# Powers of a strictly triangular matrix in a chunked linear-attention kernel: products over the part that the mask leaves

## The chip, the cores and the metric

The kernel runs on one core of one Trainium2 chip. The metric is device time in microseconds of one execution of the whole program. TensorE (PE) multiplies, VectorE (DVE) and ScalarE (ACT) move results out of PSUM and do elementwise work, GpSimd (POOL) and SyncE (SP) mostly start transfers.

## The reference

Two transformer-like layers over 4096 tokens of 256 features, fp32, one sequence:

```python
x = x + _L0_attn_ref(_layernorm(x), ...)   # linear attention with two memories
x = x + _L0_ffn_ref(_layernorm(x), ...)    # top 2 of 8 experts, 256 -> 1024 -> 256
x = x + _L1_attn_ref(_layernorm(x), ...)   # RWKV-like recurrence and channel mix
x = x + _L1_ffn_ref(_layernorm(x), ...)    # gated feed-forward, 1024 wide
```

The change is in the first attention. There each token t updates two 64x64 memories H (a fast one and a slow one, decayed by alpha) with the delta rule, and reads them with its query:

```python
d_fast = kv - k_t[:, :, None] * jnp.einsum('bk,bkv->bv', k_t, fH)[:, None, :]
fH = fast_alpha * fH + (1 - fast_alpha) * d_fast
```

## The kernel before

The attention is cut into 8 blocks of 512 tokens and each block into 4 chunks of 128 tokens: 32 chunks. Inside a chunk, token t needs what earlier tokens of the chunk wrote, which is a triangular system (1 - L) W = Y for each of the two memories (f = 0, 1). L is a 128x128 matrix, strictly lower triangular: `lower` (L595) multiplies the Gram matrix of the keys by `ncmaskT`, which is zero on and above the diagonal. The system is solved by doubling: Y becomes Y + L^(2^j) Y for j = 0 to 6, and L^(2^j) is squared between the steps. L^(2^j) has non-zero entries only where the row number is at least 2^j above the column number.

L and Y of one f lie side by side in one tile LY of 256 columns: half 0 is L, half 1 is Y. A step j of a chunk is:

- `turn(j)` (L605): PE transposes L of both f into PSUM (L608); `keep_turn` (L610) lets ACT copy it to SBUF as LT (L612, 128x256 for both f).
- `factor(j, f)` (L614): for j below 5 one product per f gives L L and L Y together, 256 columns (L619), with LT as the loaded side. For j = 5 there are two products of 128 columns: L Y (L624), and the transposed L^64 directly, with L as the loaded side and LT streaming (L627), since j = 6 needs no L itself. For j = 6 only L Y (L624).
- `keep_factor(j)` (L629): ACT copies the squared L to the next LY (L641), or, for j = 5, the transposed L^64 to an LT tile (L644); then DVE adds old and new Y (L645). For j = 6 DVE writes the sum to DP (L633).

After step 6 come a transpose of DP (`flip_d`, L650), products with the memory (`write` L663, `carry` L673) and the reads of the memory (`read` L689, L693). L609 to L612 and L639 to L645 take their tiles from rotating pools (LT 5 buffers, LY 7).

The order of the work is written out. A `Plan` collects steps with a time and a rank, sorts them, and PE, ACT, DVE and SP run exactly that order, each as one queue. A chunk begins every PACE = 7 units and its step j stands at 4 j:

```python
t = PACE * (NT * b + i) + 4 * j
for f in range(2):
    plan.at(t + f / 2, FEED, lambda j=j, f=f: factor(j, f))
plan.at(t + 1, OUT, lambda j=j: keep_factor(j))
```

So four chunks are in flight, and products of different chunks alternate on PE: between `factor(j, 0)` and `factor(j, 1)` of a chunk there is often a `turn` of another chunk. In the same queue stand the projections of later blocks (`project`; among them L442, 64 output rows, and L402, L414, L434, L453), the ends of earlier blocks (`finish`; among them the transposes L747, L781, L809 and the product L821 that contracts over 64 rows) and the routing (`route`).

Towards the end of the attention the first four slots of 256 tokens of the experts are worked on in the same plan (`full_slot`, L1088): products L1141 and L1155, then DVE adds the bias into a tile y (`add`, L1160 to L1163, two buffers) and SP stores it (L1166). The other experts follow, then the second layer.

Of the kernel before, what the change touches and what calls it, by code (L numbers as in the profile page):

```python
# [8 lines left out]
F32 = mybir.dt.float32  # L9
# [3 lines left out]
ALU = mybir.AluOpType  # L13
AX = mybir.AxisListType

P = 128
# [34 lines left out]
def mk_seq_kernel(ctx: ExitStack, tc: tile.TileContext, a: dict, out: bass.AP):  # L51
# [88 lines left out]
    def bcast(ap, shape):  # L140
        return ap.to_broadcast(shape)
# [124 lines left out]
    for q in range(3):  # L266
        t = ac.tile([P, P], F32, name=f"h{q}")
        nc.gpsimd.memset(t, 0.0)
        HS.append(t)


    TT = S // P
    sel = ac.tile([P, 2, TT, NE], F32, name="sel")
# [64 lines left out]
    ROUTE, LAST = 91, 81  # L338
    plan = Plan()
    zs = [{} for _ in range(NB)]  # L340
    memory = {"ns": None, "n": 0}

    def moments(b, z, key, i):
        if i == 0:
# [24 lines left out]
    def project(b):  # L369
# [131 lines left out]
        def starts():  # L501

            ly = z["LY"] = a2.tile([P, NT, 2, 2, P], F32, tag="LY0", name=f"LY0_{b}")
            nc.vector.tensor_tensor(
                ly[:, :, :, 1, :DS], bcast(z["KQ"][:, :, 0:1, :], [P, NT, 2, DS]),
                bcast(y["kd"].unsqueeze(3), [P, NT, 2, DS]), ALU.mult,
            )

        def values():
            nc.vector.tensor_tensor(  # L510
                z["LY"][:, :, :, 1, DS:], bcast(z["v"].unsqueeze(2), [P, NT, 2, DS]),
                bcast(z["us"].unsqueeze(3), [P, NT, 2, DS]), ALU.mult,
            )

# [51 lines left out]
    def factors(b, i):  # L566

        z = zs[b]
        y = z["c", i] = {}
        t_ = f"{b}_{i}"  # L570

        def flip():
            y["pk"] = psb([P, 2, P], f"pk_{t_}")
            for g in range(2):
                nc.tensor.transpose(
                    y["pk"][:, g, :], z["KQ"][:, i, 2 * g : 2 * g + 2, :].rearrange("p g d -> p (g d)"),
                    ident,
                )

        def keep():  # L580
            y["kq"] = a2.tile([P, 2, P], F32, tag="kqT", name=f"kqT_{t_}")
            nc.scalar.copy(y["kq"], y["pk"])

        def decayed():
            y["qT"] = a2.tile([P, P], F32, tag="qT", name=f"qT_{t_}", bufs=8)
            nc.vector.tensor_tensor(y["qT"], y["pk"][:, 1, :], qdec, ALU.mult)

        def gram():
            y["pg"] = psb([P, 2, P], f"pg_{t_}")
            nc.tensor.matmul(  # L590
                y["pg"].rearrange("p g t -> p (g t)"), y["kq"][:, 0, :],
                y["kq"].rearrange("p g t -> p (g t)"), start=True, stop=True,
            )

        def lower():  # L595
            for f in range(2):
                nc.vector.scalar_tensor_tensor(
                    z["LY"][:, i, f, 0, :], y["pg"][:, 0, :], z["us"][:, i, f : f + 1],
                    ncmaskT[:, f, :], ALU.mult, ALU.mult,
                )  # L600
            y["G"] = a2.tile([P, 2, P], F32, tag="G", name=f"G_{t_}", bufs=8)
            nc.vector.tensor_tensor(y["G"], bcast(y["pg"][:, 1:2, :], [P, 2, P]), cmask, ALU.mult)
            y["L"] = z["LY"][:, i]

        def turn(j):  # L605
            y["pt"] = psb([P, 2, P], f"pt{j}_{t_}")
            for f in range(2):
                nc.tensor.transpose(y["pt"][:, f, :], y["L"][:, f, 0, :], ident)  # L608

        def keep_turn(j):  # L610
            y["LT"] = a2.tile([P, 2, P], F32, tag="LT", name=f"LT{j}_{t_}", bufs=5)
            nc.scalar.copy(y["LT"], y["pt"])  # L612

        def factor(j, f):  # L614
            if f == 0:
                y["p"] = psa([P, 2, 2, P], f"pf{j}_{t_}")
            p, L, LT = y["p"], y["L"], y["LT"]
            if j < 5:
                nc.tensor.matmul(  # L619
                    p[:, f].rearrange("p g t -> p (g t)"), LT[:, f, :],  # L620
                    L[:, f].rearrange("p g t -> p (g t)"), start=True, stop=True,
                )
                return
            nc.tensor.matmul(p[:, f, 1, :], LT[:, f, :], L[:, f, 1, :], start=True, stop=True)  # L624
            if j == 5:

                nc.tensor.matmul(p[:, f, 0, :], L[:, f, 0, :], LT[:, f, :], start=True, stop=True)  # L627

        def keep_factor(j):  # L629
            p, L = y["p"], y["L"]  # L630
            if j == 6:
                y["DP"] = a2.tile([P, 2, 2, DS], F32, tag="DP", name=f"DP_{t_}", bufs=3)
                nc.vector.tensor_tensor(  # L633
                    y["DP"].rearrange("p g f d -> p f g d"),
                    p[:, :, 1, :].rearrange("p f (g d) -> p f g d", g=2),
                    L[:, :, 1, :].rearrange("p f (g d) -> p f g d", g=2), ALU.add,
                )
                return
            N = a2.tile([P, 2, 2, P], F32, tag="LY", name=f"LY{j + 1}_{t_}", bufs=7)  # L639
            if j < 5:  # L640
                nc.scalar.copy(N[:, :, 0, :], p[:, :, 0, :])  # L641
            else:
                y["LT"] = a2.tile([P, 2, P], F32, tag="LT", name=f"LT{j + 1}_{t_}", bufs=5)
                nc.scalar.copy(y["LT"], p[:, :, 0, :])  # L644
            nc.vector.tensor_tensor(N[:, :, 1, :], p[:, :, 1, :], L[:, :, 1, :], ALU.add)  # L645
            y["L"] = N

        def flip_d():
            y["pd"] = psb([P, P], f"pd_{t_}")
            nc.tensor.transpose(y["pd"], y["DP"][:, 0].rearrange("p f d -> p (f d)"), ident)  # L650

        def keep_d():
            y["dT"] = a2.tile([P, P], F32, tag="dT", name=f"dT_{t_}")
            nc.scalar.copy(y["dT"], y["pd"])


        def write():
            if i == 0:
                z["W"] = a2.tile([P, NT, 2, DS], F32, tag="W", name=f"W_{b}")
                z["pP"] = ps.tile([P, NT, 2, DS], F32, tag="p", name=f"pP_{b}", bufs=1)  # L660
            y["H"] = HS[memory["n"] % 3]
            y["pW"] = psc([P, P], f"pW_{t_}")
            nc.tensor.matmul(y["pW"], y["dT"], y["H"], start=True, stop=True)  # L663

        def keep_write():
            nc.vector.tensor_tensor(
                z["W"][:, i].rearrange("p f d -> p (f d)"), y["pW"],
                y["DP"][:, 1].rearrange("p f d -> p (f d)"), ALU.add,
            )

        def carry():
            y["pH"] = psc([P, P], f"pH_{t_}")
            nc.tensor.matmul(  # L673
                y["pH"], z["ke"][:, i].rearrange("p f d -> p (f d)"),
                z["W"][:, i].rearrange("p f d -> p (f d)"), start=True, stop=True,
            )

        def keep_carry():
            memory["n"] += 1
            N = HS[memory["n"] % 3]  # L680
            for f in range(2):
                o = slice(f * DS, (f + 1) * DS)
                nc.vector.scalar_tensor_tensor(
                    N[o, o], y["H"][o, o], aend[o, :], y["pH"][o, o], ALU.mult, ALU.add
                )

        def read():
            pP = z["pP"][:, i]
            nc.tensor.matmul(  # L689
                pP.rearrange("p f d -> p (f d)"), y["qT"], y["H"], start=True, stop=False  # L690
            )
            for f in range(2):
                nc.tensor.matmul(  # L693
                    pP[:, f, :], y["G"][:, f, :], z["W"][:, i, f, :], start=False, stop=(f == 1)
                )

        for t, rank, fn in (
            (-13, MIX, flip), (-12.75, OUT, keep), (-12.5, OUT, decayed), (-9, MIX, gram),
            (-8.75, OUT, lower), (-6, MIX, lambda: turn(0)), (-5.75, OUT, lambda: keep_turn(0)),
            (26, MIX, flip_d), (26.25, OUT, keep_d), (31, MIX, write), (31.25, OUT, keep_write),  # L700
            (33, MIX, carry), (33.25, OUT, keep_carry), (34, MIX, read),
        ):
            plan.at(PACE * (NT * b + i) + t, rank, fn)
        for j in range(7):
# [4 lines that stand above are left out]
            if j < 5:  # L709
                plan.at(t + 2.5, MIX, lambda j=j: turn(j + 1))  # L710
                plan.at(t + 2.75, OUT, lambda j=j: keep_turn(j + 1))
# [376 lines left out]
    def full_slot(k, ups, downs):  # L1088
# [70 lines left out]

        def add(i):  # L1160
            if i == 0:
                z["y"] = me.tile([P, NS2, D], F32, tag="y", name=f"y_f{k}", bufs=2)
            nc.vector.tensor_tensor(z["y"][:, i, :], z["px"], z["b2"], ALU.add)  # L1163

        def store():
# [1109 lines left out]
```

## Time and profile before

| what | value |
|---|---|
| three timed runs | 2042.1, 2045.76 and 2046.39 us, median 2045.76 |
| the profiled execution | 2045.78 us, span from first to last instruction 2044.3 us |
| mean granted TensorE clock in the span | 0.983 |
| L619, first to last start | 41.6 to 451.3 us |
| L624, first to last start | 61.9 to 462.6 us |
| L608, first to last start | 33.5 to 452.4 us |

The profile counts what each engine was busy with. Rows of PE are matmuls, rows of PEld the loads of their stationary side. "128*128 128x256" on a PE row means 128 contraction rows and 128 output rows, and 256 columns that stream; "64*128" contracts over 64 rows, "128*64" makes 64 output rows. A line number is that of the kernel before. Busy times of PE overlap, so the timeline's starts tell more than its durations.

### The profile page before, as it was taken

The numbers are of one execution on the slowest core, as the hardware profiler recorded it, in microseconds if no ns is written. First come the engines' busy times: TensorE is split into PE (matmuls) and PEld (weight loads), VectorE is DVE, ScalarE is ACT, GpSimd is POOL, SyncE is SP. The second block draws the span as 40 slices with busy tenths as digits, with TensorE's granted clock in tenths as the row PEclk, the third lists the DMA queues.
The fourth block names the chain that finished last, engine by engine and source line by source line (L and its number), as shares of the span: only waits on it lengthen the run. The fifth ranks groups of instructions, "written<-read, shape, count | busy, mean of one in ns | idle before, by whom it ended". The sixth has DMA issues, their size and how long they took to land. (4 is left out here: it accounts for less than half of the span.)

```text
span 2044.3 us, 27834 instructions
## 1 busy us (share of the span) xinstructions
PE 1951.9 (95%) x9879; PEld 1656.1 (81%) x9879; DVE 1244.0 (61%) x3013; ACT 1016.1 (50%) x1918; POOL 437.8 (21%) x523
## 2 busy tenths in 40 slices
PE   6999999988899999999997999999999999999998
PEld 4888777777677888888886888888888888888887
DVE  4677888876333435564635768687676876754342
ACT  3665555433222223454534656577565675744342
POOL 1000222222300012121112223232323322122121
PEclk8999999988999999999998999999999999999999
DMA  9999300023477677554433555555565555555585
GB/s 316 342 343 343 110 32 32 32 84 102 168 260 266 227 252 249 178 178 150 147 124 84 109 118 119 114 135 103 113 135 103 134 111 118 109 114 119 102 179 105
DMA packets 328856, 314.86 MB, mean 154 GB/s; under 512 B 18177, under 2 KB 308609, under 8 KB 328705
## 3 DMA queue, kind: packets, MB, share of 16 engines
q1 hardware_dynamic: 158624, 187.61, 28.1%
q0 software_dynamic: 170080, 125.33, 27.9%
q8 instruction: 83, 1.36, 0.3%
q14 instruction: 69, 0.56, 0.1%
HBM read 215.64 MB, written 97.26 MB: 153 GB/s over the span
## 5 line engine op out<-in xcount | busy, mean ns | idle before, releaser
L1086 ACT ACTIVATE hT<-peh,b 128x256 f32<-128x256 f32 x248 | 115.6, 473 | 291.3 <-PE peh L1359 285.8
L1359 PE MATMUL peh<-xgT,w 128*128 128x256 f32 x992 | 229.2, 385 | 8.6 <-DVE y L1381 6.5
L1373 PE MATMUL peo<-w,hT 128*128 128x256 f32 x992 | 224.9, 379 | 0.0
L1359 PEld LDWEIGHTS peh<-xgT,w 128*128 128x128 f32 x992 | 189.2, 193 | 38.7 <-DVE y L1381 9.4
L1932 PE MATMUL psh<-h_hi,part 128*128 128x512 f32 x512 | 211.1, 412 | 0.0
L1932 PE MATMUL psh<-sh_hi,part 128*128 128x512 f32 x512 | 209.2, 409 | 0.0
L1373 PEld LDWEIGHTS peo<-w,hT 128*128 128x128 f32 x992 | 186.7, 190 | 24.4
L2045 DVE TENSOR_TENSOR sh_lo<-hf_sh,sh_hi 128x512 fp32r<-128x512 f32 x128 | 88.3, 690 | 186.3 <-ACT sh_hi L2044 186.3
L1932 PE MATMUL psh<-h_lo,part 128*128 128x512 f32 x512 | 200.5, 392 | 0.0
L1932 PE MATMUL psh<-sh_lo,part 128*128 128x512 f32 x512 | 200.2, 391 | 0.0
L2039 ACT ACTIVATE hf_sh<-psh,vec 128x512 f32<-128x512 f32 x128 | 87.8, 686 | 225.8 <-PE psh L1932 225.4
L619 PE MATMUL pf<-LY,LT 128*128 128x256 f32 x640 | 181.1, 386 | 3.4 <-DVE LY L645 2.2
L645 DVE TENSOR_TENSOR LY<-pf,LY 128x256 f32<-128x256 f32 x192 | 79.0, 417 | 77.4 <-ACT LY L641 50.2
L619 PEld LDWEIGHTS pf<-LY,LT 128*128 128x128 f32 x640 | 106.2, 191 | 22.2 <-issue 6.3
L1827 PE MATMUL pcm<-xcT,w_cm 128*128 128x256 f32 x512 | 120.9, 379 | 0.0
L1860 PE MATMUL pcp<-k,w_cp 128*128 128x256 f32 x512 | 120.9, 379 | 0.0
L612 ACT COPY LT<-pt 128x256 f32<-128x256 f32 x192 | 71.4, 372 | 87.7 <-PE pt L608 79.2
L1932 PEld LDWEIGHTS psh<-h_lo,part 128*128 128x128 f32 x512 | 96.3, 188 | 20.1 <-DVE h_lo L2045 0.4
L1932 PEld LDWEIGHTS psh<-sh_lo,part 128*128 128x128 f32 x512 | 96.3, 188 | 19.7
L1932 PEld LDWEIGHTS psh<-sh_hi,part 128*128 128x128 f32 x512 | 96.3, 188 | 19.5
L1932 PEld LDWEIGHTS psh<-h_hi,part 128*128 128x128 f32 x512 | 96.3, 188 | 19.4
L1860 PEld LDWEIGHTS pcp<-k,w_cp 128*128 128x128 f32 x512 | 97.0, 189 | 14.9
(421 smaller groups left out, 4186.4 us busy)
## 6 DMA issues: line engine op xcount, KB each, us to landing
w<-in_w_dram SPq DMA_DIRECT2D x62, 1024.0 KB
xe_d<-zero SPq DMA_DIRECT2D x32, 1024.0 KB
ys_d<-zero SPq DMA_DIRECT2D x32, 1024.0 KB
part<-in_h1T_dram POOLq DMA_DIRECT2D x64, 512.0 KB
part<-in_h2T_dram POOLq DMA_DIRECT2D x64, 512.0 KB
w_f<-in_w_dram SPq DMA_DIRECT2D x8, 1024.0 KB
part<-in_w1T_dram POOLq DMA_DIRECT2D x32, 256.0 KB
part<-in_w2T_dram POOLq DMA_DIRECT2D x32, 256.0 KB
```

Of the source, the lines that this page charges most:

```text
L612: nc.scalar.copy(y["LT"], y["pt"])
L619: nc.tensor.matmul(p[:, f].rearrange("p g t -> p (g t)"), LT[:, f, :], L[:, f].rearrange("p g t -> p (g t)"), start=True, stop=True,)
L645: nc.vector.tensor_tensor(N[:, :, 1, :], p[:, :, 1, :], L[:, :, 1, :], ALU.add)
L1086: nc.scalar.activation(out, x, AF.Gelu_apprx_tanh, bias=bias)
L1359: nc.tensor.matmul(z["ph", h], z["w1"][:, c, h * P : (h + 1) * P], z["xT"][:, c, :], start=(c == 0), stop=(c == 1),)
L1373: nc.tensor.matmul(z["px"], z["hT"][:, h, i * P : (i + 1) * P], z["w2"][:, h, :], start=(h == 0), stop=(h == NF - 1),)
L1827: nc.tensor.matmul(pk[:, u, :], w_cm[:, c, j * P : (j + 1) * P], z["xnT"][:, c, :], start=(c == 0), stop=(c == 1),)
L1860: nc.tensor.matmul(z["pv"][:, c, :], w_cp[:, j, c * P : (c + 1) * P], z["k2"][:, g, h, u, :], start=(half == 0 and q == 0), stop=(half == ...
L1932: nc.tensor.matmul(pp, w, x[u][:, k, :], start=(k == 0 and u == 0), stop=(k == kk - 1 and u == 1))
L2039: nc.scalar.activation(h, z[nm, j], AF.Gelu, scale=col(nm, j))
L2045: nc.vector.tensor_tensor(lo[:, j, :], h, hi[:, j, :].bitcast(F32), ALU.subtract)
```

## The change

Products with a power of L leave out rows and columns that are zero. `wide(j)` is how many leading columns of L^(2^j) may be non-zero: 128 for j = 0 to 2, then 120, 112, 96, 64. LY now has Y in half 0 and L in half 1, so that the columns to be left out lie at the end. The transposed L^64 has only its upper right quarter non-zero: j = 5 computes that quarter alone (64x64), and ACT copies it into one of three lasting tiles QS whose left halves are zeroed once by POOL. In exchange for their room the tile y of `full_slot` has one buffer instead of two. The core of the diff:

```diff
+    QS = []
+    for q in range(3):
+        t = ac.tile([P // 2, 2, P], F32, name=f"q{q}")
+        nc.gpsimd.memset(t[:, :, : P // 2], 0.0)
+        QS.append(t)
...
+        def wide(j):
+            return P - 2**j if j > 2 else P
+
         def turn(j):
             y["pt"] = psb([P, 2, P], f"pt{j}_{t_}")
             for f in range(2):
-                nc.tensor.transpose(y["pt"][:, f, :], y["L"][:, f, 0, :], ident)
+                nc.tensor.transpose(y["pt"][: wide(j), f, :], y["L"][:, f, 1, : wide(j)], ident)
...
-            nc.scalar.copy(y["LT"], y["pt"])
+            nc.scalar.copy(y["LT"][: wide(j)], y["pt"][: wide(j)])
...
-            p, L, LT = y["p"], y["L"], y["LT"]
+            p, L, LT, k = y["p"], y["L"], y["LT"], wide(j)
             if j < 5:
+                n = P + wide(j + 1)
                 nc.tensor.matmul(
-                    p[:, f].rearrange("p g t -> p (g t)"), LT[:, f, :],
-                    L[:, f].rearrange("p g t -> p (g t)"), start=True, stop=True,
+                    p[:, f].rearrange("p g t -> p (g t)")[:, :n], LT[:k, f, :],
+                    L[:k, f].rearrange("p g t -> p (g t)")[:, :n], start=True, stop=True,
                 )
                 return
-            nc.tensor.matmul(p[:, f, 1, :], LT[:, f, :], L[:, f, 1, :], start=True, stop=True)
+            nc.tensor.matmul(p[:, f, 0, :], LT[:k, f, :], L[:k, f, 0, :], start=True, stop=True)
             if j == 5:
 
-                nc.tensor.matmul(p[:, f, 0, :], L[:, f, 0, :], LT[:, f, :], start=True, stop=True)
+                h = P // 2
+                nc.tensor.matmul(
+                    p[:h, f, 1, :h], L[:k, f, 1, :h], LT[:k, f, h:], start=True, stop=True
+                )
...
             if j < 5:
-                nc.scalar.copy(N[:, :, 0, :], p[:, :, 0, :])
+                nc.scalar.copy(N[:, :, 1, : wide(j + 1)], p[:, :, 1, : wide(j + 1)])
             else:
-                y["LT"] = a2.tile([P, 2, P], F32, tag="LT", name=f"LT{j + 1}_{t_}", bufs=5)
-                nc.scalar.copy(y["LT"], p[:, :, 0, :])
-            nc.vector.tensor_tensor(N[:, :, 1, :], p[:, :, 1, :], L[:, :, 1, :], ALU.add)
+                memory["q"] = memory["q"] % len(QS) + 1
+                y["LT"] = QS[memory["q"] - 1]
+                nc.scalar.copy(y["LT"][:, :, P // 2 :], p[: P // 2, :, 1, : P // 2])
+            nc.vector.tensor_tensor(N[:, :, 0, :], p[:, :, 0, :], L[:, :, 0, :], ALU.add)
...
-                z["y"] = me.tile([P, NS2, D], F32, tag="y", name=f"y_f{k}", bufs=2)
+                z["y"] = me.tile([P, NS2, D], F32, tag="y", name=f"y_f{k}")
```

The other edits swap the halves of LY in `starts`, `values`, `lower` and the last step of `keep_factor`.

More of the change, by code (lines that the diff above doesn't have):

```diff
@@ L340, in mk_seq_kernel @@
     zs = [{} for _ in range(NB)]
-    memory = {"ns": None, "n": 0}
+    memory = {"ns": None, "n": 0, "q": 0}
     def moments(b, z, key, i):
@@ L504, in starts @@
             nc.vector.tensor_tensor(
-                ly[:, :, :, 1, :DS], bcast(z["KQ"][:, :, 0:1, :], [P, NT, 2, DS]),
+                ly[:, :, :, 0, :DS], bcast(z["KQ"][:, :, 0:1, :], [P, NT, 2, DS]),
                 bcast(y["kd"].unsqueeze(3), [P, NT, 2, DS]), ALU.mult,
@@ L510, in values @@
             nc.vector.tensor_tensor(
-                z["LY"][:, :, :, 1, DS:], bcast(z["v"].unsqueeze(2), [P, NT, 2, DS]),
+                z["LY"][:, :, :, 0, DS:], bcast(z["v"].unsqueeze(2), [P, NT, 2, DS]),
                 bcast(z["us"].unsqueeze(3), [P, NT, 2, DS]), ALU.mult,
@@ L597, in lower @@
                 nc.vector.scalar_tensor_tensor(
-                    z["LY"][:, i, f, 0, :], y["pg"][:, 0, :], z["us"][:, i, f : f + 1],
+                    z["LY"][:, i, f, 1, :], y["pg"][:, 0, :], z["us"][:, i, f : f + 1],
                     ncmaskT[:, f, :], ALU.mult, ALU.mult,
@@ L634, in keep_factor @@
                     y["DP"].rearrange("p g f d -> p f g d"),
-                    p[:, :, 1, :].rearrange("p f (g d) -> p f g d", g=2),
-                    L[:, :, 1, :].rearrange("p f (g d) -> p f g d", g=2), ALU.add,
+                    p[:, :, 0, :].rearrange("p f (g d) -> p f g d", g=2),
+                    L[:, :, 0, :].rearrange("p f (g d) -> p f g d", g=2), ALU.add,
                 )
```

## The prediction

> **What bounds the kernel now.** I read the page first, then the busy times by stretch, then PE's timeline.
>
> ```profile
> span 2044.3 us, 27834 instructions
> PE 1951.9 (95%) x9879; PEld 1656.1 (81%) x9879; DVE 1244.0 (61%) x3013; ACT 1016.1 (50%) x1918; POOL 437.8 (21%) x523
> PE   6999999988899999999997999999999999999998
> PEclk8999999988999999999998999999999999999999
> ```
>
> A slice is 51 us. The lines that the change edits run from about 40 to 465 us (first and last start of L619, L624, L627): slices 1 to 9, with PE at nine tenths in most. The chain of waits only begins at 1086.65 us and so never shows this stage; but what follows it is the experts' work, PE nearly full, fed from results of this stage, so I take its lateness to be handed on whole. Busy times by stretch (columns: length, busy us and count of PE, weight loads, DVE, ACT, POOL, clock, DMA share, GB/s):
>
> ```profile
> 100.00:200.00 100.00, 97.38 (x611) 82.80 (x610) 74.54 (x230) 60.01 (x149) 8.67 (x10) 1.00 1.04 343
> 200.00:300.00 100.00, 93.95 (x578) 77.49 (x576) 79.43 (x276) 56.33 (x137) 23.16 (x23) 1.00 0.25 87
> 300.00:400.00 100.00, 93.23 (x594) 78.65 (x593) 82.43 (x281) 50.19 (x131) 22.45 (x23) 1.00 0.09 33
> ```
>
> PE leads at a full granted clock; DVE is second, ACT has room. So the stage is to be priced in PE's time from one start to the next. The timeline gives that; its first column is the start, and a PE record is longer than PE's step, since matmuls overlap. An fp32 product stands as two matmuls (L619: 640 records for 320 products), a transpose as one.
>
> ```profile
> 243.09 0.60 PE L619 MATMUL pf<-LY,LT 128*128 128x256 f32 x2
> 243.53 0.38 PE L663 MATMUL pW<-h,dT 128*128 128x128 f32 x2
> 243.75 0.39 PE L624 MATMUL pf<-LY,LT 128*128 128x128 f32 x2
> 243.97 0.38 PE L608 MATMUL pt<-ident,LY 128*128 128x128 f32 x2
> 244.19 0.39 PE L624 MATMUL pf<-LY,LT 128*128 128x128 f32 x2
> ```
>
> A matmul over 256 columns takes 0.216 us (0.44/2), over 128 columns 0.11 (0.22/2): 0.84 ns per column. The weights load meanwhile.
>
> **The price that the diff hides.** Two kinds of product are new in shape: j=6 now contracts over 64 rows, and the second product of j=5 makes 64 output rows. The kernel already has one of each: L821 contracts over 64 rows ("64*128"), L442 makes 64 rows ("128*64").
>
> ```profile
> 206.10 0.39 PE L627 MATMUL pf<-LT,LY 128*128 128x128 f32 x2
> 206.41 1.13 PE L821 MATMUL px<-w_o,oT 64*128 64x256 f32 x4
> 207.47 0.70 PE L619 MATMUL pf<-LY,LT 128*128 128x256 f32 x2
> 208.01 0.38 PE L608 MATMUL pt<-ident,LY 128*128 128x128 f32 x2
> ```
>
> L627 to L821: 0.316 instead of 0.22, so 0.094 more on entry. Four L821 take 1.06 instead of 0.864: the first is 0.104 longer (its record 480 ns, the median 376), as if its weights had not been loaded ahead, and 0.09 goes before L619 may start. L619, two matmuls, takes 0.54 instead of 0.43: again 0.104. **A visit to 64 rows costs 0.39 us.**
>
> ```profile
> 83.14 0.39 PE L624 MATMUL pf<-LY,LT 128*128 128x128 f32 x2
> 83.46 1.07 PE L442 MATMUL pn<-hn,w_nm 128*64 128x512 f32 x2
> 84.46 0.70 PE L619 MATMUL pf<-LY,LT 128*128 128x256 f32 x2
> 85.00 0.38 PE L608 MATMUL pt<-ident,LY 128*128 128x128 f32 x2
> ```
>
> Here entry costs 0.094, the two L442 take 1.00 instead of 0.858 (512 columns at 0.84 ns; 0.051 for a weight load of half the columns, 0.093 to leave), and L619 is 0.104 late: **a visit to 64 output rows costs 0.34 us.** Transposes with 64 output rows (L747: 0.11 each, neighbours unmoved) cost no visit, so the narrower transposes of the change shouldn't either.
>
> The Trainium skill, "TensorEngine Tiling (Array Packing)", section "Key Properties", says that changing the tiling mode drains TensorE, and speaks of small products as a gain from several tiles at once, which this change doesn't have. It gives no price; were a visit a drain alone (entry and leaving, 0.184 and 0.187), the sum below would be +10 us and not +33, but the rows show a bare weight load after each switch as well.
>
> **The change, part by part** (32 chunks, two f each).
>
> *j=6.* 64 products of 128 columns: contraction over fewer rows shortens nothing (L821 at 64 rows: 0.216 for 256 columns once inside). By the instruction order another chunk's transposes stand between f=0 and f=1 in 30 chunks and the two products are adjacent in 2: 62 visits x 0.392 = +24.3 us.
>
> *j=5, second product.* 128 columns become 64: two matmuls fall from 0.111 to about 0.055 (64 columns at 0.84 ns; transposes of 64 columns, L781, follow each other at 0.062), -0.114 per product. But it is a visit between 128-row outputs: +0.342. 64 x 0.228 = +14.6 us.
>
> *j=2, 3, 4.* 256 columns become 248, 240, 224, still above the weight load: 8+16+32 = 56 columns x 0.84 ns = 47 ns per f and pass; 32 x 2 x 2 x 47 ns = -6.0 us.
>
> *Transposes.* LY is the loaded side, ident's 128 columns still stream: 0.108 each as before, 0 us.
>
> *Contraction over 120, 112, 96 rows.* No row of the trace has such a shape. Ends: 0 (like 128 rows) and a visit each (like 64 rows). I take 0: 120 and 112 are nearest to 128. For the 96 rows of j=5 the upper end is one more visit per f, 64 x 0.39 = +25 us; all three, at most +75.
>
> *ACT.* Copies shrink: 128x256 took 372 ns (L644), 128x128 265 (L654), 0.83 ns per element; 16, 32, 64 and 128 elements fewer save 13+27+53+107 = 0.20 us per chunk, 6.4 us in all. DVE's add after the copy starts earlier by as much. That lies beside PE's work; worth 0 to -6.4, and I take -1 in the thinned-out end of the stage (440 to 465 us). Copying fewer partitions saves nothing: vh on 64 partitions (L420) takes 579 ns, xnT on 128 (L392) 586.
>
> *POOL.* Three memsets like L268's (0.19 us) at 3.7 us; POOL's first awaited result is needed at 7.66, cover enough; uncovered, 0.5 us.
>
> *One buffer for y_f.* The add of the next slot must await the store: adds at 518.7, 537.0 and 555.7 us follow the stores issued at 500.8, 524.8 and 545.1 by 17.9, 12.2 and 10.7 us. A 256 KB store at the 167 GB/s of that stretch is 1.6 us: 0. If a store took 5 us longer than the shortest of these gaps, three waits, +15 at the most.
>
> *Zero transposed power from a ring of three.* Its next writer comes three chunks later; 0. DVE's products have their old sizes and only trade halves.
>
> Sum on PE: 24.3 + 14.6 - 6.0 = **+32.9 us**, 1.03 us per chunk beside some 12.5 now. Not all is passed on. From 60 to 440 us PE shows 19.6 us idle, 12 of them released by DVE (L650 after L999, L633 and L737; L954 after L949; L619 after L645; L1052). DVE's load is unchanged, so a slower PE meets it less often: I take 6 us as absorbed. +32.9 - 6 - 1 = **+26 us** on the profiled execution's own 2045.78 us (span 2044.3 and 1.5 around it): **2072 us**. The median of the runs is 2045.76, the same, so the forecast stands for both.
>
> **Rivals.**
>
> *The products are simply cheaper (faster).* If neither new shape pays for a visit, because L821's and L442's price came from something else in their neighbourhood, the sum is -6.0 and at most -7.3 for j=5 (-3.6 if the next 128-column weight load bounds it), say -10, with 1 of ACT: some 2037. For it: PE's share is high, so columns do count. Against: both prices recur at every occurrence that I read. It decides if the step into j=6 stays at 0.11 us.
>
> *Only 64 contraction rows cost, 64 output rows don't.* 24.3 - 3.6 - 6.0 = +14.7, less 3: 2058. For it: L442 contracts over 128 rows, the new product over 96.
>
> *DVE is the true pace.* 82 us of 100 from 300 to 400 us; if PE's extra time mostly falls into waits for DVE's queue, I put two thirds of 33 as lost: 2056. Against: visible PE idle is 19.6 us in all, less than that.
>
> *96 rows cost a visit too.* +33 + 25, nearly all passed on: 2098.
>
> **How the numbers follow.** Forecast (both visits cost, most passed on) 0.67, at 2064 to 2082; rows alone 0.12; DVE's pace 0.07; cheaper products 0.07; 96 rows 0.07. The range leaves out the last two, 0.14: 2054 to 2084. A measurement of this kernel can tell about 0.2%, 4 us, from no change: faster 0.06, same 0.03 (edges of the second and fourth), slower 0.91.
>
> **What would show it.** After: the step before the first j=6 matmul 0.20 us instead of 0.11, and the first matmul of the next tile 0.10 late; the same at the 64x64 product; weight-load idle before both lines and before the transposes that follow. Steps of 0.19 to 0.21 us for 224 to 248 columns. PE's idle up and its last L624-like product some 25 us later than 462.6, everything after it moved by the same. I am wrong if that product ends at its old time, if the 64-row steps stay at 0.11, or if DVE's adds rather than PE end most waits.

## The result and the profile after

The changed kernel takes 2062.06 us (median of 6, 2059.74 to 2064.33), the kernel before 2043.82 (median of 6, 2040.31 to 2046.39): a ratio of 1.009, 95% interval 1.0075 to 1.0104, or 18 us slower. The forecast of 2072 had the sign right and was 10 us too high; the cause is tested below. The profiled execution took 2063.81 us.

The page of the changed kernel, the lines that answer to those of before:

```profile
span 2062.3 us, 27828 instructions
PE 1981.3 (96%) x9879; PEld 1665.2 (81%) x9879; DVE 1246.4 (60%) x3013; ACT 1010.1 (49%) x1918; POOL 438.4 (21%) x526
...
PE   6999999999988999999997999999999999999998
...
PEclk8999999996999999999999999999999999999999
```

PE has as many matmuls as before and is busy for 29 us more, in a change that only took columns and rows away. The slices that were at 8 in the attention are at 9. Busy times by stretch, the same three as in the prediction:

```profile
100.00:200.00 100.00, 98.63 (x573) 79.54 (x574) 70.40 (x211) 55.74 (x144) 7.41 (x7) 1.00 1.04 343
200.00:300.00 100.00, 96.50 (x573) 77.11 (x572) 77.16 (x266) 51.66 (x130) 23.86 (x25) 1.00 0.26 88
300.00:400.00 100.00, 96.73 (x577) 77.70 (x575) 80.39 (x266) 50.97 (x132) 15.27 (x16) 1.00 0.06 22
```

From 100 to 200 us PE starts 573 matmuls instead of 611 while it is busier, and DVE and ACT do less: the work comes through more slowly, and PE is what holds it up. The last matmul of step 6 starts at 482.4 us instead of 462.8.

PE's timeline where a chunk does its step 6 (L635 with the tile q; the first column is the start, and the time to the next start is the price):

```profile
207.91 0.39 PE L678 MATMUL pW<-h,dT 128*128 128x128 f32 x2
208.22 0.48 PE L635 MATMUL pf<-LY,q 64*128 64x128 f32 x2
208.63 0.43 PE L618 MATMUL pt<-ident,LY 128*120 128x128 f32 x2
209.00 0.48 PE L635 MATMUL pf<-LY,q 64*128 64x128 f32 x2
209.41 0.70 PE L630 MATMUL pf<-LY,LT 128*128 128x256 f32 x2
209.95 0.38 PE L618 MATMUL pt<-ident,LY 128*96 128x128 f32 x2
```

At 0.11 us per matmul of 128 columns the two L678, L635 and L618 should each take 0.22. They take 0.31 (a wait before the 64-row product), 0.41 (its weights load unhidden, and a wait after it), 0.37 (the transposes' first load unhidden, and again a wait), 0.41; then L630 needs 0.54 instead of 0.43. That the loads are unhidden shows in PE's weight loads: each of these starts with its matmul, while in the kernel before (first line) the load for the L624 at 243.75 started 0.11 us ahead of it.

```profile
243.64 0.30 PEld L624 LDWEIGHTS pf<-LY,LT 128*128 128x128 f32 x2
208.22 0.29 PEld L635 LDWEIGHTS pf<-LY,q 64*128 64x128 f32 x2
208.63 0.19 PEld L618 LDWEIGHTS pt<-ident,LY 128*120 128x120 f32 x2
209.41 0.30 PEld L630 LDWEIGHTS pf<-LY,LT 128*128 128x128 f32 x2
```

And where another chunk does step 5 (L639 is the 64x64 product):

```profile
124.19 0.39 PE L635 MATMUL pf<-LY,LT 96*128 96x128 f32 x2
124.51 0.33 PE L639 MATMUL pf<-LT,LY 96*64 96x64 f32 x2
124.77 0.44 PE L618 MATMUL pt<-ident,LY 128*128 128x128 f32 x2
125.04 0.39 PE L635 MATMUL pf<-LY,LT 96*128 96x128 f32 x2
```

0.32 instead of 0.22 to reach L639, 0.26 for two matmuls of 64 columns (0.22 had two of 128 columns before), and 0.27 instead of 0.22 for the transposes after it. The product was halved and takes longer.

### The profile page after: what moved, and what is told of

Read it like the earlier page. It is cut to its first block, busy times and chain, and to the rows that moved or that the text cites. A ratio compares the mean times of both kernels' runs of the same rounds, so it can differ in the third digit from the quotient of the medians.

```text
span 2062.3 us, 27828 instructions
## 1 busy us (share of the span) xinstructions
PE 1981.3 (96%) x9879; PEld 1665.2 (81%) x9879; DVE 1246.4 (60%) x3013; ACT 1010.1 (49%) x1918; POOL 438.4 (21%) x526
## 5 line engine op out<-in xcount | busy, mean ns | idle before, releaser
L630 PE MATMUL pf<-LY,LT 128*128 128x256 f32 (+3 forms) x640 | 178.5, 382 | 0.6 <-ACT LT L622 0.6
L622 ACT COPY LT<-pt 128x256 f32<-128x256 f32 (+3 forms) x192 | 71.3, 371 | 113.6 <-PE pt L618 112.3
L630 PEld LDWEIGHTS pf<-LY,LT 128*128 128x128 f32 (+2 forms) x640 | 106.7, 192 | 19.9 <-issue 6.4
L1947 PEld LDWEIGHTS psh<-sh_hi,part 128*128 128x128 f32 x512 | 96.2, 188 | 19.5
```

The costliest lines, as they stand in the source:

```text
L622: nc.scalar.copy(y["LT"][: wide(j)], y["pt"][: wide(j)])
L630: nc.tensor.matmul(p[:, f].rearrange("p g t -> p (g t)")[:, :n], LT[:k, f, :], L[:k, f].rearrange("p g t -> p (g t)")[:, :n], start=True, ...
L1947: nc.tensor.matmul(pp, w, x[u][:, k, :], start=(k == 0 and u == 0), stop=(k == kk - 1 and u == 1))
```

## The experiments

Each run is compared with the kernel before on the same chip in the same group. The groups ran on different chips: the kernel before had 2043.78 us in the first (E1 to E4), 2043.51 in the second (E5 to E8) and 2051.4 in the third (E9, E10), so the ratios are what can be compared across groups. "Visit" stands for what the prediction called so: one stay at a product with 64 contraction rows or 64 output rows.

### E1 to E4: the visits taken away, singly, together, and by grouping

E1, no product over 64 rows: the ring QS gets 128 rows with zeros, and step 6 uses them all.

```diff
-        t = ac.tile([P // 2, 2, P], F32, name=f"q{q}")
-        nc.gpsimd.memset(t[:, :, : P // 2], 0.0)
+        t = ac.tile([P, 2, P], F32, name=f"q{q}")
+        nc.gpsimd.memset(t, 0.0)
...
-            p, L, LT, k = y["p"], y["L"], y["LT"], wide(j)
+            p, L, LT, k = y["p"], y["L"], y["LT"], wide(j) if j < 6 else P
...
-                nc.scalar.copy(y["LT"][:, :, P // 2 :], p[: P // 2, :, 1, : P // 2])
+                nc.scalar.copy(y["LT"][: P // 2, :, P // 2 :], p[: P // 2, :, 1, : P // 2])
```

> The changed kernel, but the last power's transpose stands in tiles of 128 rows whose lower half is zero, and step 6 contracts over all 128 rows; the 64x64 product of step 5 stays. Theory of the visits (a product over 64 rows or with 64 output rows costs TensorE a drain before it, a drain after it and a weight load that nothing hides; of that about 7 tenths reach the end, the rest fills stalls that were there): the trace after shows 0.73 us of them per chunk at step 6, 23 us in all, so some 16 us less than the changed kernel, 2046 us. Rival that the 64-row products are not the main cost but the rest of the change (swapped halves, one buffer for y_f, narrower copies): less than 5 us faster than the changed kernel.

Measured: 2045.39 us, ratio 1.0013 (1.0004 to 1.0021). About 16 of the 18 us are gone with step 6's 64 rows alone.

E2, no product with 64 output rows: the second product of step 5 makes 96.

```diff
-                    p[:h, f, 1, :h], L[:k, f, 1, :h], LT[:k, f, h:], start=True, stop=True
+                    p[:k, f, 1, :h], L[:k, f, 1, :k], LT[:k, f, h:], start=True, stop=True
```

> The changed kernel, but the second product of step 5 makes 96 output rows instead of 64 (64 columns as before, the upper 64 rows are used); step 6 still contracts over 64 rows. Theory of the visits: its steps fall from 0.54 to 0.29 us per product, 64 of them, 16 us on TensorE, 7 tenths of it at the end: 2051 us. If not 64 output rows but 96 contraction rows or the short product itself cost the time, nothing changes: 2060 to 2064.

Measured: 2052.53 us, ratio 1.0039 (1.0027 to 1.0051). Half of the loss is gone. Both kinds of visit cost, each within 2 us of what the theory said.

E3, both edits.

> Both edits at once: 96 output rows in step 5 and 128 contraction rows in step 6, so that no product of the powers is narrow enough for a visit, while all columns that the mask makes zero stay left out. Theory of the visits: TensorE saves 6.0 us by 248, 240 and 224 columns and about 3 us by 64 columns against the kernel before, of which 6 or 7 tenths count: 2038 us, faster than the kernel before by 4 to 7. Rival (VectorE sets the pace, so that less TensorE time brings nothing): 2042 to 2045, the time of before. Rival (another part of the change costs): 2048 or more.

Measured: 2033.74 us, ratio 0.9955 (0.9944 to 0.9967), faster than the kernel before by 9 to 10 us, more than the theory's 4 to 7. Both rivals fall: no other part of the change shows a cost, and less PE time does bring something. PE's timeline in E3, at a step 6:

```profile
209.83 0.38 PE L678 MATMUL pW<-h,dT 128*128 128x128 f32 x2
210.05 0.39 PE L635 MATMUL pf<-LY,q 128*128 128x128 f32 x2
210.27 0.38 PE L618 MATMUL pt<-ident,LY 128*120 128x128 f32 x2
210.49 0.39 PE L635 MATMUL pf<-LY,q 128*128 128x128 f32 x2
210.72 0.50 PE L408 MATMUL pp<-w_pj,xnT 128*128 128x195 f32 x2
```

Every two matmuls are 0.22 apart. The transposes with 120 output rows stand between without any trace of a visit.

E4, the changed kernel's products in another order: both f of step 6 side by side, and the two 64x64 products of step 5 after both others.

```diff
-                plan.at(t + f / 2, FEED, lambda j=j, f=f: factor(j, f))
+                plan.at(t + (f / 2 if j < 6 else 0), FEED, lambda j=j, f=f: factor(j, f))
+            if j == 5:
+                plan.at(t + 0.5, FEED, lambda: [quarter(f) for f in range(2)])
...
```

Here `quarter(f)` is the 64x64 product of step 5, taken out of `factor`.

> The changed kernel with the same products, but the two of step 6 side by side, and the two 64x64 products of step 5 side by side after both of the others: visits to 64 rows fall from 62 to 32, to 64 output rows from 64 to 32. Theory of the visits: 0.39 and about 0.2 us per chunk less, 18 us on TensorE, some 13 at the end: 2049 us. If the price were per product and not per visit: as the changed kernel, 2060 to 2064.

Measured: 2048.16 us, ratio 1.0022 (1.0012 to 1.0032). The same products with half of the visits: three quarters of the loss is gone (more than half, since the visits that are left stand against the saved columns). The price is the visit's. PE's timeline in E4:

```profile
200.92 0.39 PE L678 MATMUL pW<-h,dT 128*128 128x128 f32 x2
201.23 0.71 PE L635 MATMUL pf<-LY,q 64*128 64x128 f32 x4
201.87 0.43 PE L618 MATMUL pt<-ident,LY 128*120 128x128 f32 x2
202.14 0.60 PE L630 MATMUL pf<-LY,LT 128*128 128x256 f32 x2
```

Four 64-row matmuls take 0.64 us, where four ordinary ones take 0.44: one unhidden load and one wait, not two of each.

### E5 and E6: a visit alone, and plain work in its stead

E5 adds the 64-row contraction to the kernel before and saves nothing; E6 makes the product of step 6 three times over.

```diff
+            k = P if j < 6 else P // 2
-            nc.tensor.matmul(p[:, f, 1, :], LT[:, f, :], L[:, f, 1, :], start=True, stop=True)
+            nc.tensor.matmul(p[:, f, 1, :], LT[:k, f, :], L[:k, f, 1, :], start=True, stop=True)
```

```diff
+            for _ in range(1 if j < 6 else 3):
                 nc.tensor.matmul(p[:, f, 1, :], LT[:, f, :], L[:, f, 1, :], start=True, stop=True)
```

> The kernel before with one edit: step 6 contracts over the first 64 rows (the others are zero), everything else as it was. No column is saved, so this is 62 visits to 64 rows by themselves. Theory of the visits: 23 us on TensorE, 7 tenths at the end: about 2060 us. If contracting over half the rows were free or a gain: 2044 or less.

> The kernel before, with the product of step 6 made three times over instead of once (the same result is written each time): 64 x 2 x 2 more matmuls of 128 columns at 0.111 us, 28 us of plain TensorE time without any visit. If some 7 tenths of whatever TensorE gets in this stage reaches the end, the rest going into waits that are there anyway: 2064 us. If only visits are taken up in part and plain work counts whole: 2072.

Measured: E5 2055.16 us, ratio 1.0059 (1.0046 to 1.0073), 12 us more with half the rows; E6 2060.37, ratio 1.0083 (1.0069 to 1.0097), 17 us more. Contracting over 64 rows is a loss by itself. But both are below the expectation: of E6's 28 us of plain work 6 tenths reach the end, of E5's 23 us of visits about half, not 7 tenths.

### E7: the shorter product of step 5

E3, with 128 columns in the second product of step 5 again.

> The kernel without visits (96 output rows, 128 contraction rows), but the second product of step 5 streams all 128 columns again; 248, 240 and 224 columns stay. By the trace of that kernel the two matmuls of the product go from 0.056 and 0.085 us to 0.11 each, 0.08 us for each of 64: 5 us on TensorE, some 3 at the end, 2037 us. Rival that the short product brings nothing, being bound by the weight load after it: as without visits, 2034.

Measured: 2035.09 us, ratio 0.9959 (0.9945 to 0.9972), beside E3's 0.9955. The intervals overlap almost wholly, so the run doesn't settle whether 64 instead of 128 columns bring 0 or 3 us.

### E8: the visits that were there before

E3, and the products that paid a visit in the kernel before are made full: `w_o` gets 64 zero rows and the tile oT 128 rows, `w_nm2` gets 64 zero columns, and the transposes of `ns` take 128 rows.

```diff
-    w_nm2 = ac.tile([P, DS], F32, name="w_nm2")
+    w_nm2 = ac.tile([P, P], F32, name="w_nm2")
+    nc.gpsimd.memset(w_nm2[:, DS:], 0.0)
...
-    w_o = ac.tile([DS, D], F32, name="w_o")
+    w_o = ac.tile([P, D], F32, name="w_o")
+    nc.gpsimd.memset(w_o[DS:], 0.0)
...
```

> The kernel without visits, and the visits that the kernel before had already are taken away as well: the output projection contracts over 128 rows with zeros below, the product with 64 output rows makes 128, and the 64-row transposes take 128 rows. By the instruction order that is 23 and 8 visits, 6.7 us of switches in 24 of the chunks by the trace and some 10 in all, less about 1.5 for the wider transposes and longer streams. Theory of the visits: 8 us less on TensorE, some 5 to 6 at the end: 2028 us, below both kernels. If the switches that were there before lay in waits: 2034, no change.

Measured: 2028.10 us, ratio 0.9926 (0.9913 to 0.9940), 15 us below the kernel before and some 6 below E3. In its timeline the line that was L821 takes 0.92 us for four matmuls, next to 1.06 in the kernel before, and the products before and after it are on time. More multiplications by zero, less time.

### E9 and E10: the single buffer, and how much of an addition passes

E9 is the kernel before with one buffer for y_f; E10 makes step 6's product twice instead of three times.

> The kernel before with one buffer instead of two for y_f and nothing else. The adds follow the store of the slot before by 10.7 to 17.9 us in the trace of before, and a store of 256 KB should take a few us: no change, 2042 to 2046 us. Rival (the single buffer is a part of the changed kernel's loss): 2048 or more.

> The kernel before with the product of step 6 made twice over instead of once: 14 us of plain TensorE time, half of what the run with three had, which came out 16.9 us later. If the waits take a share of whatever is added, 8 to 9 us: 2052. If they take a fixed stock of some 10 us before anything passes: 2047 to 2048.

Measured: E9 2049.68 us, ratio 0.9995 (0.9985 to 1.0005): the buffer costs 1 us at most. E10 2060.61, ratio 1.0040 (1.0026 to 1.0054): 8 us of 14, as much in proportion as E6's 17 of 28. A fixed stock would have left 3 to 4 us, and the interval goes from 5 to 11: the waits take a share of what is added. The share need not be constant: in the full-clock stretch that is set apart below, one profile each has some 11 of 13 us for E10 and 16 of 27 for E6.

## Why the prediction was right, and where it was off

The mechanism was right: both new shapes cost visits, and nothing else showed a cost. The size was nearer to a rival. 2062 lies inside the range of 2054 to 2084, but 2 us below the forecast's own band of 2064 to 2082; it was the rivals at 2056 and 2058 that had drawn the range so low.

*The price of a visit* was right in kind and near in size. The prediction read it off L821 and L442 and carried it to the new products. Measured in the trace after, at step 6: 0.09 before, 0.10 for the load, 0.09 after, and 0.10 at the next tile where that is L630; this is the 0.39 of the prediction. Where transposes follow, their first load shows as 0.05 and not 0.10, so the visit costs 0.34. A chunk's step 6 costs 0.73 us more (f=0 0.34, f=1 0.39), 23 us for 32 chunks, where the prediction had 24.3.

The Trainium skill, "TensorEngine Tiling (Array Packing)", "Key Properties", says that a change of tiling mode drains TensorE. No run shows whether a product over 64 rows counts as another mode; the 0.09 us on each side of it would fit. The weight loads above show that the load after a switch has to be counted too: drains alone, 62 of 0.18 us, would be 11 us on PE, and E1 got 16 back at the end.

*The 64x64 product* was priced at +0.228 us and measures +0.18 where transposes follow and +0.23 where L630 does: some 13 us for 64, predicted 14.6.

*The columns.* L630 steps at 0.209, 0.202 and 0.188 to 0.193 us for 248, 240 and 224 columns, from 0.216: 47 ns per f and pass, as predicted, -6.0 us.

*Contraction over 96, 112 and 120 rows and the narrower transposes* cost nothing: L635 over 96 rows steps at 0.11 like L624, transposes with 96 and 112 output rows at 0.109. The rival with a visit for 96 rows falls.

*The sum* on PE comes, by these prices, to 23 + 13 - 6 = +30 us against the predicted 32.9. It is really less, as a dozen of the new visits adjoin an old one (six times L836 after L639, six times L448 after L635), and the two share a switch.

*What passes on* was mis-sized, and the sum with it. The prediction took 6 us as absorbed and passed 26; the result is 18. Of the 30 us by price 6 tenths reach the end, as in E6 and E10 with plain work, which shows that it lies in the stage and not in visits. The traces show where the rest went. From the first L Y of step 5 to the product L1052 (L1067 in the changed kernel) PE makes the same 2240 matmuls in both, the visits of 30 of the 32 chunks among them, all at full clock (before, then after):

```profile
62.10:439.40 377.30, 357.77 (x2240) 301.96 (x2238) 288.25 (x952) 209.99 (x528) 62.73 (x64) 1.00 0.47 159
62.30:454.70 392.40, 380.39 (x2240) 305.69 (x2239) 290.72 (x953) 203.92 (x528) 62.82 (x64) 1.00 0.46 153
```

The stretch is 15.1 us longer. The prediction's numbers for 30 chunks would be +31 on PE and +25 passed. PE is busy for 22.6 us more and idle for 7.5 us less (19.5 to 12.0). So 8 us of the miss lie in the sum on PE, and 2 us in the idle time. Besides the shared switches, short delays that were there before can hide within PE's busy time and take up a part of a visit: of E6's 27 us of plain work in this stretch 24 show as busy time. How the 8 us split is not shown. The prediction had also named "PE's idle up" as a sign, and the visible idle time went down: a visit's waits stand in PE's busy time.

PE's waits for DVE in this stretch, before and then after (columns: who for whom, us in total, times, longest):

```profile
PE pd L650 <- DVE sg L999: 3.8, 3, 1.4
PE pfs L954 <- DVE sf L949: 2.3, 2, 1.3
PE pf L619 <- DVE LY L645: 2.2, 4, 0.6
PE pfB L1052 <- DVE slots L984: 1.8, 1, 1.8
PE pd L650 <- DVE DP L633: 1.1, 5, 0.2
PE pd L650 <- DVE er L737: 1.0, 1, 1.0
```

```profile
PE pd L665 <- DVE sg L1014: 3.3, 3, 1.4
PE pd L665 <- DVE DP L647: 1.5, 4, 1.0
PE pfB L1067 <- DVE slots L999: 1.3, 1, 1.3
PE pfs L969 <- DVE sf L964: 1.1, 2, 0.7
```

They went from 12.2 to 7.2 us; the wait for DVE's LY is gone. DVE, with the same work, is late less often for a slower PE. That is the mechanism of the rival "DVE is the true pace", in small: it took 5 us and not two thirds of 33.

The same stretch took 379.8 us in E1, 382.8 in E2, 371.2 in E3 and 389.2 in E5, one profile each (E3's has 3.4 us at half clock), so the price of the visits stands at full clock too.

*The rivals.* Cheaper products (2037): E5 rules it out, 64 rows alone lose. Rows only (2058): its time was the nearest of all to the result, yet E2 against the changed kernel shows that output rows cost as well. The forecast's mechanism and not the rival's stands, since E1 and E2 each give back a part and E3 both.

*ACT, POOL, y_f, the ring of three.* Valued at -1, 0, 0 and 0; E9 shows y_f's. E3, faster than the theory said, shows no cost of the others; one of a few us behind a larger gain is not excluded.

## What to carry to other kernels

Before rows are cut from a matmul, look at what its neighbours on PE contract over and how many output rows they make: here a product of 64 among products of 128 paid a wait on both sides and an unhidden weight load on both sides, 0.34 to 0.39 us, more than one and a half times the 0.22 us that the product itself takes. 248, 240 and 224 streamed columns took less time than 256; 120, 112 and 96 rows saved nothing, and 64 cost. So cut columns, stay at 96 rows or more or pad with zeros, and where a narrow product must be, put all of its kind side by side. And an addition to the busiest engine passes to the end only in part (here 5 to 6 tenths of its price) while that engine still waits for others now and then.

## What the runs showed of the hardware that was not expected

Multiplying by zeros was faster than leaving them out, in the kernel before too: E8 gains some 6 us over E3 by making three old products twice as large.

The weight load after a switch costs transposes 0.05 us and products 0.10, at the same 128 columns.

The granted clock at the end of the stage differs between executions. From 440 to 480 and 480 to 520 us, before and then after (the third last column is the clock):

```profile
440.00:480.00 40.00, 30.15 (x148) 24.63 (x147) 29.45 (x105) 9.10 (x21) 9.66 (x9) 0.72 0.38 119
480.00:520.00 40.00, 35.86 (x174) 28.94 (x174) 24.36 (x84) 14.45 (x26) 14.04 (x13) 0.94 0.46 152
```

```profile
440.00:480.00 40.00, 34.06 (x162) 27.79 (x160) 28.88 (x104) 10.27 (x29) 10.70 (x10) 0.69 0.38 123
480.00:520.00 40.00, 37.59 (x161) 30.80 (x162) 25.68 (x85) 10.77 (x21) 10.89 (x10) 0.72 0.21 70
```

Behind the full-clock stretch, the profiled execution after had one piece at half clock of 47.8 us; the one before had pieces of 10.2, 3.4, 10.2 and 3.4 us there.

```profile
455.00:502.80 47.80, 42.12 (x152) 34.03 (x153) 30.84 (x110) 9.38 (x22) 10.40 (x11) 0.50 0.32 102
```

The mean clocks of all runs show that this counts. E4's eleven runs go from 2042.97 us at 0.984 to 2052.47 at 0.976, some 1.2 us for 0.001. The changed kernel's six runs lie at 0.977 to 0.982 (0.979 in the mean), the 23 runs of the kernel before beside E1 to E4 at 0.981 to 0.984 (0.982). By E4's spread that is an estimated 3 to 4 us of the 18, which fits the 15.1 us of the full-clock stretch. What lowers the clock is open: E5, with visits to 64 rows, has 0.982 to 0.983, and E2, with them and the saved columns, 0.977 to 0.981.

It also bears on how E3 could gain 9 us where the step prices in its trace (6.0 for columns, and 0.056 and 0.085 us for the two matmuls of the short product instead of 0.11 each, 5 in all) sum to 11, of which 6 tenths would be 7. In the stretch up to L1067 its profile has a gain of 6 us; the rest came behind it, where E3's clock was 0.77 from 440 to 480 us and 1.00 from 480 to 520.
